# A two-layer attention kernel: v projected last, filling pieces spread from the first step to the last, and products between attention steps issued by column tiles

## The chip, the core and the metric

The kernel runs on one core of a Trainium2 chip, in float32 throughout. The metric is the device time of one execution in microseconds; a time is the median of several runs. The time before is 4138.08 us (three runs, 4136.69 to 4138.17). TensorE (`PE` in the profile) multiplies and writes to PSUM; ScalarE (`ACT`) applies functions such as Exp and copies; VectorE (`DVE`) adds, multiplies and takes reciprocals; `DMA` moves data between HBM and SBUF.

## What is computed

Sixteen images of 256 channels by 32 x 32 pixels go through two layers. An image is 1024 tokens of 256 channels.

```python
# layer 0: attention with 4 heads of 64
qkv = (xs @ w_proj + b_proj).reshape(B, S, N_HEADS, 3 * D_K)
q, k, v = jnp.split(qkv, 3, axis=-1)
attn = softmax(einsum('bihd,bjhd->bijh', q, k) * SCALE, axis=2)
res = einsum('bijh,bjhd->bihd', attn, v).reshape(B, S, N_HEADS * D_K)
res = res @ w_out + b_out + xs
# layer 1: group norm, attention with 8 heads of 32, group norm, MLP 256 -> 1024 -> 256
x = x + attention(group_norm(x, gn1_w, gn1_b), qkv_w, proj_w, proj_b, phys_bias)
h = group_norm(x, gn2_w, gn2_b)
h = gelu(einsum('oc,bchw->bohw', mlp_w1, h) + mlp_b1)
h = einsum('oc,bchw->bohw', mlp_w2, h) + mlp_b2
return x + h
```

## The kernel before

Tensors lie channels on partitions: an image is a tile `[128, 2, 1024]`. The keys of a block of 128 tokens, as the stationary operand, meet 512 query columns, so scores come out transposed, keys on partitions. Exp is taken straight from PSUM without a maximum; its result is the moving operand of the weighted sum with v. A test at the end of the kernel on the sums (`in_range`) decides whether a general, slower second pass is needed. It isn't with these inputs.

An attention runs in steps. A step computes the scores of one to three (item, key block) units, `s_a` in layer 0 and `s_b` in layer 1, and hands them to ScalarE for Exp; then it issues the weighted sums `acc_a` or `acc_b` of the step before. Each head takes its own rows of TensorE in the scores (D of 128) and its own columns in the weighted sums (D of 128), with D 64 in layer 0 and 32 in layer 1.

```python
        per = 6 // G                       # G = 128 // D heads side by side
        ...
        def scores(i, kb):
            t, c = items[i]
            tiles = [wide(f"s_{key}_{i}_{kb}_{n}") for n in range(G // 2)]
            for g in range(G):
                nc.tensor.matmul(          # L252
                    tiles[g // 2][:, g % 2, :],
                    kT[g * D : (g + 1) * D, c, kb * P : (kb + 1) * P],
                    qT[g * D : (g + 1) * D, c, t * TB : (t + 1) * TB],
                    start=True, stop=True,
                )
            ...
                nc.scalar.activation(e, s, AF.Exp, scale=scale)      # L264
        def weigh(i, kb, es):
            ...
            for g in range(G):
                nc.tensor.matmul(          # L273
                    accs[i][g * D : (g + 1) * D, :],
                    v_of(c * G + g, kb),
                    es[g // 2][:, g % 2, :],
                    start=(kb == 0), stop=(kb == SB - 1),
                )
            ...
                nc.vector.tensor_add(d, held[i][n] if kb == 1 else d, e)   # L290
        ...
        pending = []
        for step in steps:
            now = [scores(*u) for u in step]
            for p in pending:
                weigh(*p)
            pending = now
            yield
        for p in pending:
            weigh(*p)
        yield
```

`normalise` adds up the denominators with a product of ones (`den_a`, `den_b`, L300, also D columns wide) and divides. The PSUM tiles `wide` (two banks) rotate over three buffers: scores, projections and MLP outputs all take them in turn. `bank` tiles have two buffers.

The projections to q, k and v are six pieces, each with a `wide` tile. ScalarE takes q and k out of PSUM, VectorE takes v out.

```python
        def qk(ch, which, dst):
            ps = wide(f"qk_{key}_{ch}_{which}")      # four products 128 x 128 x 512, L406
            ...
        def v(half):
            ps = wide(f"v_{key}_{half}")             # eight products 128 x 128 x 256, L428
            ...
        pieces = [
            lambda: qk(0, 1, kT), lambda: qk(0, 0, qT), lambda: v(0), lambda: v(1)
        ]
        for ch in range(1, CC):
            pieces.append(lambda ch=ch: qk(ch, 1, kT))
            pieces.append(lambda ch=ch: qk(ch, 0, qT))
        return pieces
```

The driver fills the steps of the second attention of image b with whole pieces of other work: the eight pieces of the MLP's second product of image b-1 (`m`, L534, eight products of 128 x 128 x 256 each) and the six projection pieces of image b+1's first attention. `later.tick()` issues work that was put off by some steps: denominators, the output projections (`o`, `j`, L336) and the parts of group norm. Layer 1's own projections and the MLP's first product (`m`, L517) run outside the attentions' steps or after the first attention's last ones.

```python
    def run(stage, fill=None):
        for n, _ in enumerate(stage):
            later.tick()
            if fill and n in fill:
                fill[n]()
    ...
        fill = outputs + (first_qkv if b > 0 else [])
        tiles1, second_qkv = qkv_1(b, xn)
        run_pieces(second_qkv)
        hn = act.tile([P, CC, S], F32, tag="gn", name=f"hn_{b}")
        run(
            attention_1(...),
            {2 * n + 2: piece for n, piece in enumerate(fill)},
        )
        hidden, outputs = mlp(b, xs[b], hn)
```

The second attention has 32 units in steps of one, so steps 0 to 31 and a last one for the last weighted sums. With 14 pieces the places were steps 2, 4 ... 28; image 0 has none, image 15 has the eight `m` pieces alone.

Of the kernel before, what the change touches and what calls it, by code (L numbers as in the profile page):

```python
# [14 lines left out]
P = 128  # L15
# [175 lines left out]
def first_pass(ctx, tc, x, out, k):  # L191
    nc = tc.nc
    B, C, S = x.shape
    CC, SB, NT = C // P, S // P, S // TB
# [33 lines left out]

# [4 lines left out]
    def attention(layer, b, D, qT, kT, v_of, ones_of, scale, project):  # L238
        key = f"{layer}_{b}"
        G = P // D  # L240
        items = [(t, c) for t in range(NT) for c in range(CC)]
        units = [(i, kb) for i in range(len(items)) for kb in range(SB)]
        per = 6 // G
        steps = [units[n : n + per] for n in range(0, len(units), per)]
        res = act.tile([P, CC, S], F32, tag="res", name=f"res_{key}")
        accs, held, sums = {}, {}, {}
# [9 lines that stand above are left out]
                    start=True,  # L256
                    stop=True,
                )
            es = []
            for n, s in enumerate(tiles):  # L260
                e = work.tile(
                    [P, 2, TB], F32, tag="e", name=f"e_{key}_{i}_{kb}_{n}", bufs=8
                )
                nc.scalar.activation(e, s, AF.Exp, scale=scale)  # L264
                es.append(e)
            return i, kb, es

        def weigh(i, kb, es):
            t, c = items[i]
            if kb == 0:  # L270
                accs[i] = bank(f"acc_{key}_{i}")
# [5 lines that stand above are left out]
                    start=(kb == 0),  # L277
                    stop=(kb == SB - 1),
                )
            if kb == 0:  # L280
                held[i] = es
                return
            if kb == 1:
                sums[i] = [
                    work.tile([P, 2, TB], F32, tag="es", name=f"es_{key}_{i}_{n}", bufs=4)
                    for n in range(G // 2)
                ]
            for n, e in enumerate(es):
                d = sums[i][n]
                nc.vector.tensor_add(d, held[i][n] if kb == 1 else d, e)  # L290
            if kb == SB - 1:
                r = res[:, c, t * TB : (t + 1) * TB]
                nc.scalar.copy(r, accs.pop(i))
                later.after(2, lambda: normalise(i, r))

        def normalise(i, r):
            t, c = items[i]
            den = bank(f"den_{key}_{i}")
            for g in range(G):
                nc.tensor.matmul(  # L300
                    den[g * D : (g + 1) * D, :],
                    ones_of(c * G + g),
                    sums[i][g // 2][:, g % 2, :],
                    start=True,
                    stop=True,
                )
            at = next(block)
            d = work.tile([P, TB], F32, tag="d", name=f"d_{key}_{i}", bufs=1)
            nc.scalar.activation(  # L309
                d, den, AF.Identity, accum_out=dsum[:, at : at + 1]  # L310
            )
            nc.scalar.activation(
                den, den, AF.Exp, scale=-1.0 / DEN_MIN, accum_out=lsum[:, at : at + 1]
            )
            nc.vector.reciprocal(d, d)  # L315
            nc.vector.tensor_mul(r, r, d)
            if c == CC - 1:
                later.after(3, lambda: project(t, res))

        pending = []  # L320
        for step in steps:
            now = [scores(*u) for u in step]
# [4 lines that stand above are left out]
        for p in pending:  # L327
            weigh(*p)
        yield


    def out_proj(key, w, nk, src, bias, xs, t, stats):
        ps = wide(f"{key}_{t}")
        for co in range(CC):
            for kc in range(nk):
                nc.tensor.matmul(  # L336
                    ps[:, co, :],
                    w[:, kc, co * P : (co + 1) * P],
                    src(kc),
                    start=(kc == 0),  # L340
                    stop=(kc == nk - 1),
                )
        for co in range(CC):
            y = xs[:, co, t * TB : (t + 1) * TB]
            nc.vector.scalar_tensor_tensor(
                y, ps[:, co, :], bias[:, co : co + 1], y, ALU.add, ALU.add
            )
            if stats is not None:
                nc.vector.bn_stats(stats[:, co, t, :], y)


    def group_norm(key, src, stats, gw, gb, y):
# [10 lines left out]

        def variances():
            ps = bank(f"gm_{key}")
            nc.tensor.matmul(ps[:, :CC], k["gavg"], st["mean_c"], start=True, stop=True)
            mean = small.tile([P, CC], F32, tag="mean", name=f"mean_{key}")
            nc.vector.tensor_copy(mean, ps[:, :CC])

            dv = small.tile([P, CC], F32, tag="dv", name=f"dv_{key}")  # L370
            nc.vector.tensor_sub(dv, st["mean_c"], mean)
            nc.vector.tensor_mul(dv, dv, dv)
            tv = small.tile([P, CC], F32, tag="tv", name=f"tv_{key}")
            nc.vector.tensor_add(tv, dv, st["mv"][:, :, 1])
            st.update(mean=mean, tv=tv)
            later.after(1, apply)

        def apply():
            ps = bank(f"gv_{key}")
            nc.tensor.matmul(ps[:, :CC], k["gavg"], st["tv"], start=True, stop=True)  # L380
            rstd = small.tile([P, CC], F32, tag="rstd", name=f"rstd_{key}")
            nc.vector.tensor_scalar(rstd, ps[:, :CC], EPS, None, ALU.add)
            nc.gpsimd.tensor_tensor(rstd, rstd, k["mhalf"], ALU.pow)
            a = small.tile([P, CC], F32, tag="ga", name=f"ga_{key}")
            nc.vector.tensor_mul(a, rstd, gw)
            ma = small.tile([P, CC], F32, tag="gma", name=f"gma_{key}")
            nc.vector.tensor_mul(ma, st["mean"], a)
            c = small.tile([P, CC], F32, tag="gc", name=f"gc_{key}")
            nc.vector.tensor_sub(c, gb, ma)
            for t in range(NT):  # L390
                sl = slice(t * TB, (t + 1) * TB)
                for cc in range(CC):
                    nc.vector.tensor_scalar(  # L393
                        y[:, cc, sl], src[:, cc, sl],
                        a[:, cc : cc + 1], c[:, cc : cc + 1], ALU.mult, ALU.add,
                    )
# [4 lines left out]
    def qkv(key, D, src, weights, b_qk, b_v, v_op, qT, kT, v_dst):  # L401
        def qk(ch, which, dst):
            ps = wide(f"qk_{key}_{ch}_{which}")
            for t in range(NT):
                for cc in range(CC):
                    nc.tensor.matmul(  # L406
                        ps[:, t, :],
                        weights(cc, which)[:, ch * P : (ch + 1) * P],
                        src[:, cc, t * TB : (t + 1) * TB],
                        start=(cc == 0),  # L410
                        stop=(cc == CC - 1),
                    )
# [8 lines left out]
        def v(half):  # L421
            ps = wide(f"v_{key}_{half}")
            n = SB // 2
            for i in range(n):
                sb = half * n + i
                o = ps[:, i // 2, (i % 2) * C : (i % 2 + 1) * C]
                for cc in range(CC):
                    nc.tensor.matmul(  # L428
                        o,
                        src[:, cc, sb * P : (sb + 1) * P],  # L430
                        weights(cc, 2),
# [8 lines left out]
                v_op,  # L440
            )

        pieces = [
            lambda: qk(0, 1, kT), lambda: qk(0, 0, qT), lambda: v(0), lambda: v(1)
        ]
        for ch in range(1, CC):
            pieces.append(lambda ch=ch: qk(ch, 1, kT))
            pieces.append(lambda ch=ch: qk(ch, 0, qT))
        return pieces

    def qkv_0(b, xb):
        q = act.tile([P, CC, S], F32, tag="q0", name=f"q0_{b}")
# [56 lines left out]
    def mlp(b, xb, hn):  # L509
# [20 lines left out]
        def reduce(t, co, half):  # L530
            n = TB // 2
            ps = wide(f"m2_{b}_{t}_{co}_{half}")[:, 0, :n]
            for hc in range(HC):
                nc.tensor.matmul(  # L534
                    ps,
                    k["w2"][:, hc, co * P : (co + 1) * P],
                    gs[t, hc][:, half * n : (half + 1) * n],
# [42 lines left out]
    for b in range(B):  # L580
# [12 lines left out]
        if b + 1 < B:  # L593
            tiles0, first_qkv = qkv_0(b + 1, xs[b + 1])
        run_pieces(first_qkv if b == 0 else hidden)
        later.flush()
        fill = outputs + (first_qkv if b > 0 else [])
        tiles1, second_qkv = qkv_1(b, xn)
        run_pieces(second_qkv)
        hn = act.tile([P, CC, S], F32, tag="gn", name=f"hn_{b}")  # L600
# [4 lines left out]
                    f"h{b}", xs[b], st, k["g2w"], k["g2b"], hn  # L605
                ),
            ),
            {2 * n + 2: piece for n, piece in enumerate(fill)},
        )
        hidden, outputs = mlp(b, xs[b], hn)  # L610
    later.flush()
# [296 lines left out]
```

## Time and profile before

| what | value |
|---|---|
| time, median of 3 | 4138.08 us |
| span of the profiled run | 4135.9 us |
| mean granted TensorE clock | 0.992 |
| PE busy | 4072.8 us, 18,817 matmuls |
| DVE busy | 2489.1 us |
| ACT busy | 2082.1 us |
| second attention, Exp (L264, `e_b`) | 1024 of 1022 ns |
| second attention, sums of Exp (L290, `es_b`) | 896 of 1216 to 1222 ns |
| `m`, 128 x 256 columns (L534) | 2048 matmuls, 474.7 us busy |
| data moved by DMA | 40.90 MB, mean 10 GB/s |

A line of a group names the source line, engine and operation, what is written from what, the shape (rows * columns of the stationary operand, then partitions x elements of the moving one) and the count; then busy time and mean duration of one; then the idle time just before such instructions and who ended it. Matmuls overlap, so their mean durations add up to more than their busy time. On the timeline equal instructions in a row are merged into one line: start, length, count, and in brackets the idle time before with its releaser. The end of a matmul is modelled, so differences between starts are the safer measure.

### The profile page before, as it was taken

How to read it: one execution, taken by the hardware profiler on the slowest of the kernel's cores; microseconds unless marked ns; L12 is line 12 of the kernel's file. 1: busy time of each engine (PE TensorE's matmuls, PEld its weight loads, DVE VectorE, ACT ScalarE, POOL GpSimd, SP SyncE). 2: the span in 40 equal slices, each digit the busy share in tenths (PEclk: the TensorE clock that was granted, in tenths of full speed). 3: DMA queues.
4: the chain of work that ended last, by engine and by line, in shares of the span. 5: the costliest groups of instructions: out<-in, count | busy, mean ns of one | idle time of the engine just before them, and what ended most of it. 6: DMA issues, size and time to landing. Idle time of an engine off the chain costs nothing.

```text
span 4135.9 us, 45760 instructions
## 1 busy us (share of the span) xinstructions
PE 4072.8 (98%) x18817; PEld 1689.5 (41%) x18817; DVE 2489.1 (60%) x2538; ACT 2082.1 (50%) x2623; POOL 32.7 (1%) x54
## 2 busy tenths in 40 slices
PE   9999999999999999999999999999999999999998
PEld 3334344343443434434344343443434434344344
DVE  4684746747467474664746647466574665737563
ACT  4564545545455454554545545454454544645452
POOL 1000000000000000000000000000000000000000
PEclk9999999999999999999999999999999999999999
DMA  2000000000000000000000000000000000000000
GB/s 73 1 1 8 13 1 21 1 8 13 1 21 1 8 13 1 21 1 13 9 3 19 1 21 1 3 19 1 21 1 3 19 1 21 1 6 6 0 11 11
DMA packets 19800, 40.90 MB, mean 10 GB/s; under 512 B 5216, under 2 KB 6752, under 8 KB 19584
## 3 DMA queue, kind: packets, MB, share of 16 engines
q1 hardware_dynamic: 13824, 33.56, 2.2%
q10 hardware_dynamic: 5296, 4.20, 0.4%
q8 instruction: 149, 2.44, 0.2%
q14 instruction: 67, 0.55, 0.0%
q0 software_dynamic: 464, 0.15, 0.0%
HBM read 21.12 MB, written 16.78 MB: 9 GB/s over the span
## 4 chain that ended last, share of the span: by engine, by line
PE 91%; DVE 4%; ACT 2%; issue 2%; DMA 0%; POOL 0%; ACTq 0%; POOLq 0%; DVEq 0%
PE s_b L252 12%; PE acc_a L273 11%; PE m L517 11%; PE s_a L252 11%; PE acc_b L273 11%; PE m L534 10%; PE qk_a L406 6%; PE qk_b L406 5%; PE v_a L428 3%; PE o L336 3%; PE j L336 3%; PE v_b L428 3%; DVE es_b L290 2%; DVE d_b L315 2%; PE den_a L300 1%
## 5 line engine op out<-in xcount | busy, mean ns | idle before, releaser
L264 ACT ACTIVATE e_b<-s_b 128x1024 f32<-128x1024 f32 x1024 | 990.8, 1022 | 635.5 <-PE s_b L252 620.9
L290 DVE TENSOR_TENSOR es_b<-es_b,e_b 128x1024 f32<-128x1024 f32 x768 | 894.5, 1216 | 256.9 <-ACT e_b L264 256.4
L252 PE MATMUL s_b<-q,k 32*128 32x512 f32 x4096 | 647.3, 652 | 26.0 <-ACT e_b L264 18.1
L264 ACT ACTIVATE e_a<-s_a 128x1024 f32<-128x1024 f32 x512 | 488.6, 1024 | 199.0 <-PE s_a L252 168.7
L273 PE MATMUL acc_b<-e_b,v 128*32 128x512 f32 x4096 | 570.4, 615 | 1.6
L252 PE MATMUL s_a<-q,k 64*128 64x512 f32 x2048 | 490.9, 608 | 0.0
L290 DVE TENSOR_TENSOR es_a<-es_a,e_a 128x1024 f32<-128x1024 f32 x384 | 467.3, 1217 | 36.7 <-ACT e_a L264 10.6
L273 PE MATMUL acc_a<-e_a,v 128*64 128x512 f32 x2048 | 478.3, 601 | 0.0
L517 PE MATMUL m<-hn,w 128*128 128x512 f32 x1024 | 474.7, 605 | 2.0 <-DVE hn L393 2.0
L534 PE MATMUL m<-g,w 128*128 128x256 f32 x2048 | 474.7, 385 | 0.0
L534 PEld LDWEIGHTS m<-g,w 128*128 128x128 f32 x2048 | 379.1, 190 | 149.4 <-issue 66.9
L252 PEld LDWEIGHTS s_b<-q,k 32*128 32x128 f32 x4096 | 200.5, 186 | 398.5 <-issue 260.7
L525 ACT ACTIVATE g<-m,m1b 128x512 f32<-128x512 f32 x256 | 170.2, 685 | 314.2 <-PE m L517 313.8
L252 PEld LDWEIGHTS s_a<-q,k 64*128 64x128 f32 x2048 | 181.8, 186 | 282.0 <-issue 250.3
L290 DVE TENSOR_TENSOR es_b<-e_b,e_b 128x1024 f32<-128x1024 f32 x128 | 151.1, 1222 | 237.4 <-ACT e_b L264 237.4
L517 PEld LDWEIGHTS m<-hn,w 128*128 128x128 f32 x1024 | 186.0, 190 | 256.3 <-issue 190.7
L315 DVE RECIPROCAL d_a<-d_a 128x512 f32<-128x512 f32 x64 | 214.6, 3353 | 86.0 <-ACT d_a L309 86.0
L273 PEld LDWEIGHTS acc_a<-e_a,v 128*64 128x64 f32 x2048 | 131.3, 136 | 325.3 <-issue 320.7
L273 PEld LDWEIGHTS acc_b<-e_b,v 128*32 128x32 f32 x4096 | 83.0, 108 | 413.9 <-issue 385.4
L406 PE MATMUL qk_a<-x,wp 128*128 128x512 f32 x512 | 237.7, 608 | 8.1 <-DMA wp<-in_L_conv_w_proj_dram 8.1
L406 PE MATMUL qk_b<-xn,wq 128*128 128x512 f32 x512 | 229.2, 596 | 2.3 <-DVE xn L393 2.3
L315 DVE RECIPROCAL d_b<-d_b 128x512 f32<-128x512 f32 x64 | 214.2, 3346 | 2.7 <-ACT d_b L309 2.7
(104 smaller groups left out, 2290.5 us busy)
## 6 DMA issues: line engine op xcount, KB each, us to landing
x<-in_x_dram SPq DMA_DIRECT2D x32, 512.0 KB, 4.4
out_dram<-x SPq DMA_DIRECT2D x64, 256.0 KB, 2.0
w<-in_L_conv_mlp_w_dram ACTq DMA_DIRECT2D x2, 1024.0 KB, 11.4
wp<-in_L_conv_w_proj_dram ACTq DMA_DIRECT2D x6, 128.0 KB, 8.2
wq<-in_L_conv_qkv_w_dram ACTq DMA_DIRECT2D x1, 768.0 KB, 10.4
wo<-in_L_conv_w_out_dram ACTq DMA_DIRECT2D x1, 256.0 KB, 5.4
wpj<-in_L_conv_proj_w_dram ACTq DMA_DIRECT2D x1, 256.0 KB, 10.8
bv<-in_L_conv_b_proj_dram POOLq DMA_DIRECT2D x1, 128.0 KB, 8.0
```

The source lines that it names most:

```text
L252: nc.tensor.matmul(tiles[g // 2][:, g % 2, :], kT[g * D : (g + 1) * D, c, kb * P : (kb + 1) * P], qT[g * D : (g + 1) * D, c, t * TB : (t + ...
L264: nc.scalar.activation(e, s, AF.Exp, scale=scale)
L273: nc.tensor.matmul(accs[i][g * D : (g + 1) * D, :], v_of(c * G + g, kb), es[g // 2][:, g % 2, :], start=(kb == 0), stop=(kb == SB - 1),)
L290: nc.vector.tensor_add(d, held[i][n] if kb == 1 else d, e)
L300: nc.tensor.matmul(den[g * D : (g + 1) * D, :], ones_of(c * G + g), sums[i][g // 2][:, g % 2, :], start=True, stop=True,)
L315: nc.vector.reciprocal(d, d)
L336: nc.tensor.matmul(ps[:, co, :], w[:, kc, co * P : (co + 1) * P], src(kc), start=(kc == 0), stop=(kc == nk - 1),)
L406: nc.tensor.matmul(ps[:, t, :], weights(cc, which)[:, ch * P : (ch + 1) * P], src[:, cc, t * TB : (t + 1) * TB], start=(cc == 0), stop=(cc ...
L428: nc.tensor.matmul(o, src[:, cc, sb * P : (sb + 1) * P], weights(cc, 2), start=(cc == 0), stop=(cc == CC - 1),)
L517: nc.tensor.matmul(ps[:, n, :], k["w1"][:, cc, hc * P : (hc + 1) * P], hn[:, cc, t * TB : (t + 1) * TB], start=(cc == 0), stop=(cc == CC - 1),
L525: nc.scalar.activation(g, ps[:, n, :], AF.Gelu, bias=k["m1b"][:, hc : hc + 1])
L534: nc.tensor.matmul(ps, k["w2"][:, hc, co * P : (co + 1) * P], gs[t, hc][:, half * n : (half + 1) * n], start=(hc == 0), stop=(hc == HC - 1),)
```

## The change

Three things are changed. First, the projection pieces come in the order k, q, k, q, v, v instead of k, q, v, v, k, q, in both layers. Second, the pieces that fill the second attention stand evenly from step 0 to step 31, the last at step 31: with 14 pieces at 0, 2, 4, 7, 9 ... 28, 31. Third, while an attention's steps run, every other product goes through a helper that cuts the stationary operand's 128 columns into tiles of D columns, the width of the weighted sums, so that consecutive groups keep one shape of TensorE's array. Outside of the steps the helper issues full products as before.

```diff
+    cols = [P]
+
+    def product(o, w, r, **flags):
+        for c0 in range(0, P, cols[0]):
+            sl = slice(c0, c0 + cols[0])
+            nc.tensor.matmul(o[sl], w[:, sl], r, **flags)
 ... in attention()
+        cols[0] = D
         pending = []
         for step in steps:
 ...
             weigh(*p)
         yield
+        cols[0] = P
 ... in out_proj, in group_norm's two averages, in qk, in v and in the MLP's reduce
-                nc.tensor.matmul(
+                product(
 ... in qkv()
-        pieces = [
-            lambda: qk(0, 1, kT), lambda: qk(0, 0, qT), lambda: v(0), lambda: v(1)
-        ]
-        for ch in range(1, CC):
+        pieces = []
+        for ch in range(CC):
             pieces.append(lambda ch=ch: qk(ch, 1, kT))
             pieces.append(lambda ch=ch: qk(ch, 0, qT))
-        return pieces
+        return pieces + [lambda: v(0), lambda: v(1)]
 ... in the loop over images
+        last = NT * CC * SB - 1
-            {2 * n + 2: piece for n, piece in enumerate(fill)},
+            {n * last // max(len(fill) - 1, 1): piece for n, piece in enumerate(fill)},
```

More of the change, by code (lines that the diff above doesn't have):

```diff
@@ L365, in variances @@
             ps = bank(f"gm_{key}")
-            nc.tensor.matmul(ps[:, :CC], k["gavg"], st["mean_c"], start=True, stop=True)
+            product(ps[:, :CC], k["gavg"], st["mean_c"], start=True, stop=True)
             mean = small.tile([P, CC], F32, tag="mean", name=f"mean_{key}")
@@ L379, in apply @@
             ps = bank(f"gv_{key}")
-            nc.tensor.matmul(ps[:, :CC], k["gavg"], st["tv"], start=True, stop=True)
+            product(ps[:, :CC], k["gavg"], st["tv"], start=True, stop=True)
             rstd = small.tile([P, CC], F32, tag="rstd", name=f"rstd_{key}")
@@ L405, in qk @@
                 for cc in range(CC):
-                    nc.tensor.matmul(
+                    product(
                         ps[:, t, :],
@@ L427, in v @@
                 for cc in range(CC):
-                    nc.tensor.matmul(
+                    product(
                         o,
@@ L533, in reduce @@
             for hc in range(HC):
-                nc.tensor.matmul(
+                product(
                     ps,
```

## The prediction, made before the changed kernel was run

> **What bounds the kernel now.** I read the page first: the busy shares, the chain that ended last, and the costliest groups. `PE` is TensorE's matmuls, `PEld` its weight loads; a group line gives the shape of one instruction, the count, and then the busy time and the mean ns of one.
>
> ```profile
> PE 4072.8 (98%) x18817; PEld 1689.5 (41%) x18817; DVE 2489.1 (60%) x2538; ACT 2082.1 (50%) x2623; POOL 32.7 (1%) x54
> PE 91%; DVE 4%; ACT 2%; issue 2%; DMA 0%; POOL 0%; ACTq 0%; POOLq 0%; DVEq 0%
> L252 PE MATMUL s_b<-q,k 32*128 32x512 f32 x4096 | 647.3, 652 | 26.0 <-ACT e_b L264 18.1
> L273 PE MATMUL acc_b<-e_b,v 128*32 128x512 f32 x4096 | 570.4, 615 | 1.6
> ```
>
> TensorE is the bound: 98% busy, 91% of the chain. But 98% is not 98% useful. The count of matmul records is twice that of the program, so each float32 product is two passes. A pass over 512 columns takes 0.43 us: the steady weight loads of `qk_b` start at 2142.97, 2143.40, 2143.83 us. A pass over 256 columns takes 0.216 us: 30 of `v_b` between 2132.63 and 2139.11. Four of `acc_b`'s 32-column tiles, or four of `s_b`'s 32-row tiles, run at once, so eight of either are 0.86 us of work. All passes of the program so counted come to some 3,630 us, against 4,136 of span. The missing 500 us lie inside "busy", so I went to the timeline of TensorE over one middle image (columns: start, length, engine, line, operation). The images repeat every 256 us.
>
> ```profile
> 2211.12 1.06 PE L273 MATMUL acc_b<-e_b,v 128*32 128x512 f32 x8
> 2212.12 3.72 PE L534 MATMUL m<-g,w 128*128 128x256 f32 x16
> 2215.77 1.14 PE L252 MATMUL s_b<-q,k 32*128 32x512 f32 x8
> 2216.84 1.06 PE L273 MATMUL acc_b<-e_b,v 128*32 128x512 f32 x8
> 2217.72 1.04 PE L300 MATMUL den_b<-es_b,eones 128*32 128x512 f32 x8
> 2218.69 1.14 PE L252 MATMUL s_b<-q,k 32*128 32x512 f32 x8
> ```
>
> Read differences of starts, since ends are modelled. `acc_b` takes 1.00 us when a group of another shape follows and 0.88 when `den_b`, also 128*32, follows: leaving a shape costs 0.12. `m` takes 3.65 where 16 passes are 3.46: 0.19, about 0.10 for its first weights, which nothing hid, and 0.09 for leaving. So a group of full products put between the steps of an attention costs 0.19 us more than its passes, and the `acc_b` before it pays for leaving either way (scores would follow, also another shape).
>
> The second loss stands at both ends of the second attention.
>
> ```profile
> 2146.07 2.30 PE L252 MATMUL s_b<-q,k 32*128 32x512 f32 x12
> 2146.17 1.01 ACT L415 COPY q<-qk_b 128x1024 f32<-128x1024 f32 x1 [2.42 <-PE qk_b L406]
> 2147.20 1.28 ACT L264 ACT_TABLE_LOAD   x1
> 2148.50 3.77 ACT L264 ACTIVATE e_b<-s_b 128x1024 f32<-128x1024 f32 x4
> 2149.57 1.13 PE L252 MATMUL s_b<-q,k 32*128 32x512 f32 x4 [1.21 <-ACT e_b L264]
> 2150.63 1.83 PE L273 MATMUL acc_b<-e_b,v 128*32 128x512 f32 x8
> 2152.39 2.02 PE L252 MATMUL s_b<-q,k 32*128 32x512 f32 x8
> 2154.34 1.07 PE L273 MATMUL acc_b<-e_b,v 128*32 128x512 f32 x8
> ```
>
> The last `q` is copied out by ScalarE after the scores have begun, then the table for Exp is loaded, and only at 2148.50 does the first Exp run. The three score buffers are full and TensorE waits. From the first scores to the first filling piece (2155.33) are 9.26 us. The same 40 matmuls at their usual pace are 1.93 (sixteen scores in one go) + 1.00 + 1.07 + 1.00 = 5.00, so 4.26 us are lost.
>
> ```profile
> 2272.65 1.14 PE L252 MATMUL s_b<-q,k 32*128 32x512 f32 x8
> 2273.72 3.15 PE L273 MATMUL acc_b<-e_b,v 128*32 128x512 f32 x16
> 2276.80 2.85 PE L252 MATMUL s_a<-q,k 64*128 64x512 f32 x12
> ```
>
> At the end the last two steps' weighted sums take 3.08 us where 16 matmuls need 1.86 (0.43 x 4, 0.02, 0.12 for leaving): 1.22 us wait for the last Exps, with no piece left to fill.
>
> **What the Trainium skill says.** "TensorEngine Tiling (Array Packing)", Key Properties: a change of tiling mode, not of tile alone, drains the engine. The trace agrees: 0.12 us between `acc_b` and `m`, none between `acc_b` and `den_b`. "TensorE: Matmul & The Clock Gate", The mechanism: tiles in separate column groups run concurrently, a few ns apart. It agrees: eight `acc_b` of 615 ns each pass in 0.88 us. The same page, under "Wait — 56ns, not 53.3ns?", has matmuls start no closer than about 25 ns, however small; no run here comes near that, and it decides a rival below. "ScalarE: Activation LUTs", What ACT_TABLE_LOAD costs: about 1283 ns for the load itself; the trace has 1.28 us.
>
> **The change part by part**, per image of the regular kind (images 1 to 14), from the order of the built program and the rows above.
>
> (1) Column tiles. Within an attention every other product is cut into tiles of 32 columns (second attention) or 64 (first), the shape of the weighted sums. The matmul count rises fourfold or twofold, but the tiles run together, so I keep the pass times: a piece of `m` or `v_a` stays 16 x 0.216 = 3.46, one of `qk_a` or `j` 8 x 0.43 = 3.44. In the second attention 14 gaps per image held such products (`j` shared one). Each loses its 0.19 to 0.20 us: 14 x 0.196 = 2.74. Piece 0 now stands after the first scores with no weighted sum before it; where scores would have followed scores freely, there are two changes of shape, 0.35 us by the rows above (0.11 + 0.02 + 0.11 + 0.10). Net **2.4 us**. In the first attention `o` (between two weighted sums), `j` and one of group norm's small averages save 0.33 + 0.20 + 0.2: **0.7 us**.
>
> (2) v last. The order becomes k0, q0, k1, q1, v0, v1. ScalarE's last copy, and with it the table load, now come some 7 us (two `v_b` pieces of 3.46) before the first scores, and VectorE takes v out. Then Exp starts at once after the first scores, and piece 0 occupies TensorE for 3.46 us meanwhile. What stays is piece 0's buffer: it is that of v1, which VectorE frees 1.23 us (its eviction) after v1's end, while the first scores last 1.07 us: a wait of 0.2 to 0.4. The steady wait of 0.2 for a score group that no piece precedes (2209.88 to 2211.12 is 1.24 against 1.07) also stays. Gain 4.26 - 0.3 - 0.2 = **3.75 us**.
>
> (3) Last piece at step 31. It falls between the two last weighted sums, same shape on both sides, and covers the wait for the last Exps: **1.2 us**. The pieces are 2.4 steps apart instead of 2, so one more score group goes without a piece before it: **-0.2**.
>
> Sum: 2.4 + 0.7 + 3.75 + 1.2 - 0.2 = 7.85 us, times 14 images = 110. Image 0 has no pieces in its second attention and no table load there (1.4 us of wait before its first weighted sum): some 2, with a 1.3 us stall of `v_a` at 21.8 us in the first projection. Image 15 has eight pieces, all used by step 16 before and now spread to the end: about 7, by the same terms and part of the 2.99 us wait for `es_b` in the tail. Together about 119: 4138 - 119 = 4019. I say 4022, as small waits that I can't see only add.
>
> **Rivals.**
> A. Instruction supply. A tiled piece of 256 columns is 64 matmuls and 64 weight loads in 3.46 us, 27 ns for each instruction. The densest stretch in the trace, `acc_b` then `den_b`, is 32 in 1.85 us, 58 ns each, so nothing shows the rate needed. For it: group norm's `gv_g`, met with an empty queue, loads weights at 1604.12 and 1604.22 and the next ones follow at 1604.33; a pair per 0.105 us is an upper limit of 53 ns per instruction, and the matmul at 1604.15, 0.03 us after its load, hints at 30. At 53 ns ten pieces an image would each take 2 to 3 us longer: 20 to 30 us x 15, about 4,350 us. At 40 ns the gain of part 1 and more is gone, some 4,080.
> B. Tiles that don't overlap over a long chain. `acc_a` shows six pairs of passes at 0.43 each with two tiles, but chains of 16 with four tiles that read one moving operand are nowhere. If they ran even 10% slower, 14 x 0.35 = 5 us an image are lost: about 4,095.
> C. VectorE takes over the end. It needs 2 x 1.22 us per step in the second attention, and it evicts v1 and the last `m` just where buffers are scarce. Against it: 60% busy, and pieces spread evenly give it more time per step (2.4 x 2.1 + 3.5 = 8.5 us for 5.9 of sums). If it holds the first attention's third buffer, 1 us an image, 4,035.
> D. Only the order matters and the tiles neither gain nor cost: (2) and (3) alone, 4.75 x 14 + 8 = 75, 4,063.
>
> **Range and chances.** The gain from order (75 us, 1.8%) rests on waits that the timeline shows; the tiles add 45 us if their passes keep their pace. The limit for faster by over 2% is 4,055. Most of what can go wrong is A and B, which reach from 4,060 to 4,350; that the sum is too small by 25 us I also allow. Range 3,992 to 4,095; faster 0.68, within 0.20, slower 0.12.
>
> **What will show it.** In the timeline of a middle image: `acc_b` to a piece 0.88 us instead of 1.00; a piece of tiled `m` 3.46 to 3.6 instead of 3.65 to the next scores (if 4 or more, A or B); ACT_TABLE_LOAD before the first scores and the first weighted sum at its usual pace; from the first to the last scores no wait over 0.4 us; 16 `acc_b` at the end no longer one group of 3.08. An image then repeats every 248 us instead of 256. PEld's and PE's counts rise by some 9,100 (4,570 more products of two passes in the built program) to about 28,000, with little more busy time. The prediction is wrong if tiled pieces last longer than full ones, or if scores wait for VectorE's evictions of v.

## The result, and the profile after

The changed kernel takes 4013.68 us (median; 4011.88 to 4015.50), against 4137.91 before (the median of four executions now): a ratio of 0.970, 95% interval 0.9684 to 0.9717, or 124 us less. The prediction was 4022, range 3992 to 4095.

The page of the changed kernel has these lines, in the order in which the prediction read those of before (busy us, share, matmuls; then the chain; then two groups).

```profile
PE 3971.1 (99%) x27957; PEld 1518.4 (38%) x27957; DVE 2481.6 (62%) x2538; ACT 2078.1 (52%) x2623; POOL 32.7 (1%) x54
PE 94%; DVE 4%; issue 1%; ACT 0%; DMA 0%; POOL 0%; ACTq 0%; POOLq 0%; DVEq 0%
L262 PE MATMUL s_b<-q,k 32*128 32x512 f32 x4096 | 624.3, 640 | 2.8 <-DVE x L552 1.3
L236 PE MATMUL m<-g,w 128*32 128x256 f32 (+1 forms) x7808 | 464.9, 379 | 3.7 <-DVE v L448 3.7
```

There are 9,140 matmuls more and 102 us less of busy TensorE; ScalarE has left the chain (2% to 0%). The tiled `m` has four times the records, and about the same busy time as the full `m` had (474.7 us). All products that go through the helper carry its line, L236; the MLP's first product doesn't and keeps its own. The images repeat every 247.83 us (the second attention of images 7 and 8 begins at 1843.10 and 2090.93 us) where it was 255.97 (1890.10 and 2146.07).

The timeline of TensorE in the middle of the second attention, as before:

```profile
2099.21 1.06 PE L283 MATMUL acc_b<-e_b,v 128*32 128x512 f32 x8
2100.10 3.64 PE L236 MATMUL m<-g,w 128*32 128x256 f32 x64
2103.66 1.14 PE L262 MATMUL s_b<-q,k 32*128 32x512 f32 x8
2104.73 1.07 PE L283 MATMUL acc_b<-e_b,v 128*32 128x512 f32 x8
2105.73 1.37 PE L262 MATMUL s_b<-q,k 32*128 32x512 f32 x8
```

By starts, `acc_b` before `m` takes 0.89 us, about what it took before `den_b`; it still takes 1.00 before scores (2104.73 to 2105.73). `m` takes 3.56 to the next scores instead of 3.65: the change of shape on its way out, to the scores, is still paid.

The start of the second attention, with ScalarE and VectorE beside TensorE:

```profile
2084.13 1.01 ACT L427 COPY q<-qk_b 128x1024 f32<-128x1024 f32 x1 [2.42 <-PE qk_b L236]
2085.16 1.28 ACT L274 ACT_TABLE_LOAD   x1
2090.93 1.14 PE L262 MATMUL s_b<-q,k 32*128 32x512 f32 x8
2091.03 1.22 DVE L448 TENSOR_TENSOR v<-v_b,eones 128x1024 f32<-128x1024 f32 x1 [2.23 <-PE v_b L236]
2092.31 3.66 PE L236 MATMUL m<-g,w 128*32 128x256 f32 x64 [0.25 <-DVE v L448]
2095.91 1.14 PE L262 MATMUL s_b<-q,k 32*128 32x512 f32 x8
2096.98 1.06 PE L283 MATMUL acc_b<-e_b,v 128*32 128x512 f32 x8
```

The table load has ended four microseconds before the first scores, piece 0 follows them and waits 0.25 us for v's eviction, and the first weighted sum stands at its usual distance of 1.07 us from the second scores. At the end the two last weighted sums are parted by the last piece:

```profile
2208.78 1.07 PE L283 MATMUL acc_b<-e_b,v 128*32 128x512 f32 x8
2209.66 3.64 PE L236 MATMUL v_a<-wp,x 128*32 128x256 f32 x64
2213.11 1.04 PE L283 MATMUL acc_b<-e_b,v 128*32 128x512 f32 x8
2214.08 2.85 PE L262 MATMUL s_a<-q,k 64*128 64x512 f32 x12
```

The piece takes 3.45 us, its bare passes; the sums take 0.88 and 0.97. Nothing waits.

### The profile page after: what moved, and what is told of

Same layout as the page of the kernel before. It is cut to its first block, busy times and chain, and to the rows that moved or that the text cites. A ratio compares the mean times of both kernels' runs of the same rounds, so it can differ in the third digit from the quotient of the medians.

```text
span 4013.6 us, 64073 instructions
## 1 busy us (share of the span) xinstructions
PE 3971.1 (99%) x27957; PEld 1518.4 (38%) x27957; DVE 2481.6 (62%) x2538; ACT 2078.1 (52%) x2623; POOL 32.7 (1%) x54
## 4 chain that ended last, share of the span: by engine, by line
PE 94%; DVE 4%; issue 1%; ACT 0%; DMA 0%; POOL 0%; ACTq 0%; POOLq 0%; DVEq 0%
PE s_b L262 14%; PE acc_b L283 12%; PE m L527 11%; PE m L236 11%; PE s_a L262 11%; PE acc_a L283 11%; PE qk_a L236 6%; PE qk_b L236 6%; PE o L236 3%; PE v_b L236 3%; PE v_a L236 3%; PE j L236 3%; PE den_a L310 1%; PE den_b L310 1%; DVE d_a L325 1%
## 5 line engine op out<-in xcount | busy, mean ns | idle before, releaser
L262 PE MATMUL s_b<-q,k 32*128 32x512 f32 x4096 | 624.3, 640 | 2.8 <-DVE x L552 1.3
L283 PE MATMUL acc_b<-e_b,v 128*32 128x512 f32 x4096 | 546.1, 604 | 0.0
L527 PE MATMUL m<-hn,w 128*128 128x512 f32 x1024 | 476.1, 606 | 2.0 <-DVE hn L405 2.0
L236 PE MATMUL m<-g,w 128*32 128x256 f32 (+1 forms) x7808 | 464.9, 379 | 3.7 <-DVE v L448 3.7
L236 PEld LDWEIGHTS m<-g,w 128*32 128x32 f32 (+1 forms) x7808 | 272.6, 111 | 227.7 <-issue 59.3
L527 PEld LDWEIGHTS m<-hn,w 128*128 128x128 f32 x1024 | 186.6, 191 | 257.1 <-issue 191.5
L448 DVE TENSOR_TENSOR v<-v_b,eones 128x1024 f32<-128x1024 f32 x32 | 39.2, 1224 | 394.4 <-PE v_b L236 394.4
L236 PE MATMUL qk_a<-x,wp 128*32 128x512 f32 (+1 forms) x1856 | 234.3, 594 | 9.1 <-DMA wp<-in_L_conv_w_proj_dram 9.1
L236 PE MATMUL qk_b<-xn,wq 128*128 128x512 f32 x512 | 226.6, 596 | 3.3 <-DVE xn L405 3.3
```

Of the source, the lines that this page charges most:

```text
L236: nc.tensor.matmul(o[sl], w[:, sl], r, **flags)
L262: nc.tensor.matmul(tiles[g // 2][:, g % 2, :], kT[g * D : (g + 1) * D, c, kb * P : (kb + 1) * P], qT[g * D : (g + 1) * D, c, t * TB : (t + ...
L283: nc.tensor.matmul(accs[i][g * D : (g + 1) * D, :], v_of(c * G + g, kb), es[g // 2][:, g % 2, :], start=(kb == 0), stop=(kb == SB - 1),)
L448: nc.vector.tensor_tensor(v_dst[:, half * n : (half + 1) * n], ps.rearrange("p a (b h d) -> p (a b) h d", b=2, d=D), b_v.unsqueeze(1).to_b ...
L527: nc.tensor.matmul(ps[:, n, :], k["w1"][:, cc, hc * P : (hc + 1) * P], hn[:, cc, t * TB : (t + 1) * TB], start=(cc == 0), stop=(cc == CC - 1),
```

## The experiments

| run | median us | ratio to before | 95% interval |
|---|---|---|---|
| the change | 4013.68 | 0.9700 | 0.9684 to 0.9717 |
| tiles_alone | 4093.29 | 0.9892 | 0.9875 to 0.9908 |
| order_alone | 4065.29 | 0.9823 | 0.9806 to 0.9839 |
| no_v_last | 4027.47 | 0.9734 | 0.9718 to 0.9750 |
| no_spread | 4066.25 | 0.9829 | 0.9812 to 0.9845 |
| tiles_64 | 4045.47 | 0.9773 | 0.9758 to 0.9788 |
| narrow_128 | 4026.93 | 0.9729 | 0.9711 to 0.9746 |
| all_tiled | 4055.70 | 0.9798 | 0.9780 to 0.9816 |
| halves | 4050.74 | 0.9783 | 0.9770 to 0.9797 |
| qk_halves | 4016.33 | 0.9705 | 0.9692 to 0.9718 |
| qk_halves_v_mid | 4014.54 | 0.9700 | 0.9686 to 0.9713 |
| qk_halves_full | 4071.36 | 0.9839 | 0.9824 to 0.9854 |
| v_last_first_only | 4010.65 | 0.9688 | 0.9675 to 0.9702 |

All compute everything that the reference does. Edits are against the changed kernel. narrow_128 and all_tiled have two executions each, the others four or five. The kernel before took 4137.79 to 4139.79 beside them, so a difference of 2 us between two of these medians says nothing by itself.

### The parts by themselves

**tiles_alone**

```diff
-        return pieces + [lambda: v(0), lambda: v(1)]      # k q k q v v
+        return pieces                                     # k q v v k q, as before
-            {n * last // max(len(fill) - 1, 1): piece for n, piece in enumerate(fill)},
+            {2 * n + 2: piece for n, piece in enumerate(fill)},
```

> The change's column tiles alone, with the order of pieces and their places as before. Theory T (a change of the array's shape costs 0.19 to 0.20 us per gap, and tiles of the weighted sums' width avoid it): 14 gaps x 0.196 = 2.7 us per image in the second attention and 0.7 in the first, 3.4 x 14.5 = some 50 us, so 4088; the waits at the start (4.26 us) and end (1.22 us) of the second attention stay. Rival D (only the order matters): 4138. Were the tiles to run slower than full products, over 4138.

Measured 4093.29: 44.5 us less than before (4137.79 on that chip), where theory T had 50. Rival D, that only the order matters, falls. In the trace the waits at both ends stay as they were: 9.10 us from the first scores to the first piece (1871.52 to 1880.62), and one group of 3.08 us for the last weighted sums.

**order_alone**

```diff
-        cols[0] = D
+        cols[0] = P
```

> v last and pieces from step 0 to step 31, with full products of 128 columns everywhere. Theory T: the change less 3.4 us per image, 4014 + 50 = 4064; acc_b before m takes 1.00 us again, m 3.65 to the next scores. If the tiles gave nothing: 4014. If the two parts depend on each other (piece 0 and piece 31 cost more with two changes of shape, 0.3 us each): up to 4070.

Measured 4065.29, one microsecond from theory T's number. So the order is worth 72.5 us by itself and the tiles 51.6 on top of it. The two parts alone sum to 117 of the change's 124: they depend on each other little, by some 7 us. Its timeline at the end shows one place where they do: the last piece, full, between two weighted sums.

```profile
2238.61 1.07 PE L283 MATMUL acc_b<-e_b,v 128*32 128x512 f32 x8
2239.61 3.72 PE L236 MATMUL v_a<-wp,x 128*128 128x256 f32 x16
2243.26 1.06 PE L283 MATMUL acc_b<-e_b,v 128*32 128x512 f32 x8
```

1.00 + 3.65 us by starts, against 0.88 + 3.45 with tiles: 0.32 for the two changes of shape, in and out, with the first weights.

**no_v_last** and **no_spread** take one half of the reordering away each, and keep the tiles.

```diff
 no_v_last:
-        return pieces + [lambda: v(0), lambda: v(1)]
+        return pieces                                     # k q v v k q
 no_spread:
-            {n * last // max(len(fill) - 1, 1): piece for n, piece in enumerate(fill)},
+            {2 * n + 2: piece for n, piece in enumerate(fill)},
```

> The change without v last: tiles, and pieces from step 0 to 31, but k, q, v, v, k, q. Theory V (the prediction's step 2: v last frees the start of the second attention): the table load and the last copy of q stand again between the first scores and the first Exp, 2.3 us, so some 2 to 3.5 us per image are lost and the time is 4045 to 4065. Rival P (piece 0, which now stands right after the first scores and lasts 3.46 us, covers that wait by itself; v last then only replaces ScalarE's eviction by VectorE's before piece 0): within 0.3 us per image of the change, 4009 to 4019.

> The change with v last and tiles, but the pieces at steps 2, 4 ... 28 as before. Theory V: the start is nearly free, a wait of 1 to 1.5 us for the third buffer and the first Exps, and only the end's 1.2 us come back: 4014 + 14 x 2 = 4042. Rival P (piece 0 does the work at the start): the start loses 3 us or more, 4014 + 14 x 4.2 = 4073 or above.

Measured 4027.47 and 4066.25: neither theory's number in either case. The timelines say why. The start of the second attention without v last:

```profile
2096.63 1.14 PE L262 MATMUL s_b<-q,k 32*128 32x512 f32 x8
2097.76 1.28 ACT L274 ACT_TABLE_LOAD   x1
2097.80 3.66 PE L236 MATMUL m<-g,w 128*32 128x256 f32 x64
2101.39 1.14 PE L262 MATMUL s_b<-q,k 32*128 32x512 f32 x8
2102.46 1.06 PE L283 MATMUL acc_b<-e_b,v 128*32 128x512 f32 x8
```

The table load is back between the first scores and the first Exp, and costs nothing: from the first scores to the first weighted sum are 5.83 us, against 6.05 with v last. Rival P holds for the start; piece 0 covers the wait by itself. The 14 us of this run are lost elsewhere, late in the same attention:

```profile
2197.25 3.34 DVE L325 RECIPROCAL d_b<-d_b 128x512 f32<-128x512 f32 x1
2197.54 3.64 PE L236 MATMUL v_a<-wp,x 128*32 128x256 f32 x64
2203.32 1.21 DVE L448 TENSOR_TENSOR v<-v_a,bv 128x1024 f32<-128x1024 f32 x1
2204.59 1.14 PE L262 MATMUL s_b<-q,k 32*128 32x512 f32 x8 [1.35 <-DVE v L448]
```

With v in the middle, one `v_a` piece falls just after a block's denominators. VectorE divides for 3.34 us, has sums of Exp queued behind, and takes v out of PSUM 2.2 us after the piece's end (2201.11 to 2203.32); the scores that need that buffer wait 1.35 us. The trace has 14 such waits, 18.9 us in all; less the gain of 0.22 at each start that is 15.8, about the 14 measured.

In no_spread, v last alone brings the stretch from the first scores to the first piece from 9.10 us (tiles_alone) to 6.26 (2112.35 to 2118.61), of which 4.88 are work, the 5.00 less 0.12 that the tiles save. So v last takes 2.8 of some 4.2 us at the start, piece 0 takes all of it, and together they overlap. What this run loses, an image repeating every 251.11 us (1861.24 to 2112.35), is 3.3 us: the end's 1.2 (the last weighted sums are one group of 3.08 us again), some 0.7 at the start, and a wait of 1.27 us for an eviction of v behind a reciprocal, for the places of the pieces decide that too. Times 14 this is 46 of the 53 us; in the tail a wait of 3.0 us for `es_b` is back as well.

### What a change of shape costs

**tiles_64**

```diff
-        cols[0] = D
+        cols[0] = 64
```

> The change with products cut into tiles of 64 columns in the second attention too, where the weighted sums have 32. Theory T (a change of shape is what costs): each of about 14 gaps pays again 0.115 us for leaving the weighted sums' shape and 0.05 for the first weights of 64 columns, the last piece, between two weighted sums, 0.3: 2.4 us per image, 4014 + 34 = 4048. Rival (cutting in itself helps, for instance because narrow weights load quicker): within 8 us of the change.

Measured 4045.47, 32 us above the change, 3 from theory T. The timeline has the change's wait and the full products' one apart:

```profile
2116.05 1.07 PE L283 MATMUL acc_b<-e_b,v 128*32 128x512 f32 x8
2117.05 3.67 PE L236 MATMUL m<-g,w 128*64 128x256 f32 x32
2120.65 1.14 PE L262 MATMUL s_b<-q,k 32*128 32x512 f32 x8
```

1.00 us before a tile of another width, as before a full product; 3.60 for the piece, between the full product's 3.65 and the 3.56 of 32 columns. That the width of the first weights makes this small difference fits, but was not tested apart. It is the equal shape that pays, not the cutting.

### Whether tiles keep their pace

**narrow_128**: the MLP's second products on 128 moving columns.

```diff
-            for hc in range(HC):
-                product(ps, ..., gs[t, hc][:, half * n : (half + 1) * n], ...)
+            for z in range(2):
+                for hc in range(HC):
+                    product(ps[:, z * P : (z + 1) * P], ...,
+                            gs[t, hc][:, half * n + z * P : half * n + (z + 1) * P], ...)
```

> The change with the MLP's second products issued on 128 moving columns instead of 256, twice as many: 256 instructions per piece where the passes need 3.46 us, 13.5 ns each. It measures the rate at which instructions can be supplied and weights loaded (rival A). If neither limits: 4014. If the weight loads of some 110 ns set the pass: 32 passes of 0.11, +0.1 us a piece, 4026. If instructions come at 25 to 30 ns each: 256 of them take 6.4 to 7.7 us less a few queued ahead, +2.5 to 4 us a piece, 120 pieces: 4310 to 4500. At 53 ns: above 5,000.

Measured 4026.93. A piece:

```profile
2104.28 3.68 PE L236 MATMUL m<-g,w 128*32 128x128 f32 x128
2107.88 1.14 PE L262 MATMUL s_b<-q,k 32*128 32x512 f32 x8
```

128 matmuls and as many weight loads in 3.60 us are 14 ns for each instruction, twice the rate that the change needs, at 0.04 us more per piece. Rival A is out. Half of a 256-column pass would be 0.108 us, and a narrow weight load lasts 110 ns here, so the passes can't tell whether the loads would limit. The 13 us over the change fit the number for limiting loads, but only 5 of them lie in the pieces. The other 8 are waits of the scores for VectorE: 11.1 us in the trace (9.6 of them for `x`, the eviction of `m`) against 2.8 in the change. So the agreement with the number 4026 is largely chance.

**all_tiled**: tiles of 32 columns also outside of the attentions' steps.

```diff
-    cols = [P]
+    cols = [32]
-        cols[0] = P
+        cols[0] = 32
```

> The change with every helped product in 32-column tiles outside of the attentions too, so that long unbroken chains of tiled products stand in the trace: the v projections of the second attention (256 instructions in 6.9 us) and the last image's MLP (28 us). Rival B (long chains of tiles lag) or A (supply) would show passes of more than 0.216 us there: 0.25 would make v_b 8 us instead of 7. Theory T: the passes keep 0.216 and 0.43, and the time is the change's, plus up to 16 x 0.6 us for new changes of shape in the hidden stage: 4014 to 4025.

Measured 4055.70, above theory T's range. The pace isn't the reason. The longest unbroken chain, the last image's MLP, as far as the view goes (to 4048 us):

```profile
4022.27 26.10 PE L236 MATMUL m<-g,w 128*32 128x256 f32 x479
```

is 120 passes of four tiles in 26 us, 0.217 us each; rival B is out as well. What costs is the stage between the attentions, where the MLP's first product (L527) stays full and the scheduler mixes `o`, `qk_b` and group norm's averages into it: from the last weighted sum of the first attention to the first scores of the second it takes 59.02 us instead of 56.16. That is 2.86 us, nearly five times my allowance of 0.6; times 16 it is 46, for the 42 measured.

Besides changes of shape, single tiles cost here. Two of the scheduler's groups hold one column tile of a product alone:

```profile
2088.59 1.04 PE L236 MATMUL qk_b<-xn,wq 128*32 128x512 f32 x2
2089.56 1.98 PE L527 MATMUL m<-hn,w 128*128 128x512 f32 x4
```

Two matmuls are the two passes of one tile out of four, and they take 0.97 us, about what the whole product takes in the change (0.94, 2068.29 to 2069.23). The other three tiles follow after `m` and need the time again. `o` has the same at 2066.75. Two passes of 0.43 us lost twice are by estimate 1.7 of the 2.86 us. The tile that was put ahead keeps its lead to the end of `qk_b`:

```profile
2102.66 2.32 PE L236 MATMUL qk_b<-xn,wq 128*32 128x512 f32 x19
2104.40 0.59 PE L236 MATMUL v_b<-wq,xn 128*32 128x256 f32 x2
2104.80 0.60 PE L236 MATMUL qk_b<-xn,wq 128*32 128x512 f32 x3
2104.83 7.49 PE L236 MATMUL v_b<-wq,xn 128*32 128x256 f32 x126
```

It begins `v_b` 0.4 us before the other three have begun their last pass of `qk_b`, and doesn't wait for them. From its start `v_b` lasts 7.85 us (to the scores at 2112.25), which looks like the 8 us of rivals A and B. But the other three tiles can begin only at 2104.80 + 0.43 = 2105.23, and from there it is 7.02, where full products took 7.00. The pace is kept, and the lead is worth nothing, since the scores wait for the last tile.

### Finer pieces

**halves**, **qk_halves**, **qk_halves_v_mid**, **qk_halves_full**: the projection pieces in the second attention cut in two. halves cuts all six, qk_halves only those of q and k. qk_halves_v_mid is qk_halves (the "last run" of its text) with v in the middle in the second layer's own projections; qk_halves_full is qk_halves with full products.

```diff
-            for t in range(NT):
+            nt = NT // parts                         # parts = 2 for images from 2 on
+            ts = range(part * nt, (part + 1) * nt)
+            for t in ts:
 halves:
-        return pieces + [lambda: v(0), lambda: v(1)]
+        return pieces + [lambda half=half: v(half) for half in range(2 * parts)]
 qk_halves_v_mid:
+        at = 2 if D == D1 else len(pieces)
+        return pieces[:at] + [lambda: v(0), lambda: v(1)] + pieces[at:]
 qk_halves_full:
-        cols[0] = D
+        cols[0] = P
```

> The change with the six projection pieces that fill the second attention cut in halves (twelve of 1.72 us), so that 20 of 32 steps have a piece instead of 14. With tiles a gap costs nothing, so more gaps are free, and a score group that a piece precedes does not wait for its buffer (1.07 us against 1.24 to 1.30). Theory: 5 to 6 more score groups without the wait of 0.2, 1 us per image for images 1 to 14: 4000, less some for evictions in halves, which have a fixed part. If the wait for buffers is only moved: 4014.

Measured 4050.74, 37 us slower than the change instead of 14 faster. The halves of v begin earlier and meet a reciprocal again:

```profile
2216.77 3.35 DVE L325 RECIPROCAL d_b<-d_b 128x512 f32<-128x512 f32 x1
2222.84 0.68 DVE L451 TENSOR_TENSOR v<-v_a,bv 128x512 f32<-128x512 f32 x1
2223.58 1.93 PE L236 MATMUL v_a<-wp,x 128*32 128x256 f32 x32 [2.46 <-DVE v L451]
```

The next half waits 2.46 us for the buffer of the first, whose eviction stood behind the division, a multiplication and two additions. The trace has 14 such waits, 34.5 us of the 37.

> As in the run with halves, but only the four q and k pieces are cut in two and v stays whole and last, so that v's eviction no longer falls behind a reciprocal of 3.35 us on VectorE. Theory (that eviction was the loss; cutting as such gains): 18 pieces instead of 14, four more score groups at 1.07 instead of 1.24 us, 0.7 us per image: 4014 - 10 = 4004. Rival (more evictions on ScalarE cost what the gaps bring): 4014 or above.

Measured 4016.33. The loss of halves is gone, so that reading of it stands, but the gain of 10 us hasn't come either. The number is the rival's, but that evictions on ScalarE ate the gain is not shown. The timeline of the middle images gives another reason: of two score groups in a row without a piece only the first waits (in the change 2205.41 to 2206.71 is 1.30 us, the next, 2207.70 to 2208.78, 1.08). Parting such pairs by more pieces leaves the number of waiting groups much as it was: in one middle image's 32 score groups, 14 last over 1.1 us in the change and 15 in qk_halves. My count of gaps was not the count of waits.

> The last run, with v back in the middle for the second layer's own projections alone, where no reciprocal is in the way. The run without v last showed the start of the second attention 0.2 us shorter with v in the middle, since ScalarE frees piece 0's buffer sooner than VectorE: 0.22 x 15 = 3 us, 4001. Rival (the start needs v last after all): 4015 or above.

Measured 4014.54, 1.8 us below its sibling, with intervals that overlap; in the traces an image is 0.2 us shorter (247.96 against 248.17).

> The run with q and k in halves, with full products in place of tiles. Theory T: each of the four more gaps now costs two changes of shape, 0.2 us more, and saves a wait of 0.17: nothing is won, within 5 us of the order alone with full products, 4065. Rival (cutting pays whatever the shape): 4055.

Measured 4071.36, 6 us above the order alone with full products. As theory T has it, finer pieces win nothing there; they lose a little, one microsecond more than it allowed.

**v_last_first_only**

```diff
-        return pieces + [lambda: v(0), lambda: v(1)]
+        at = 2 if D == D1 else len(pieces)
+        return pieces[:at] + [lambda: v(0), lambda: v(1)] + pieces[at:]
```

> The change, but v last only in the first layer's projections, which fill the second attention; the second layer's own order is k, q, v, v, k, q again. If piece 0 alone frees the start of the second attention and v last pays only at the other place, by keeping v's eviction away from the reciprocals: the start gets 0.22 us shorter as in the run without v last, no 1.4 us wait comes back, 14 x 0.22 = 3 us less than the change: 4010 to 4012. If v last is needed at the start: 4016 or more.

Measured 4010.65, as piece 0's theory has it, and the fastest of all. Its interval overlaps the change's. In its trace an image repeats every 247.61 us (1839.82 to 2087.43), 0.22 less than in the change, and the first weighted sum stands 5.84 us after the first scores (2087.43 to 2093.27). v last has no use in the second layer's own projections; it has one in the pieces that fill the second attention.

## Why the prediction was right, point by point

- **TensorE's shape changes (step 1).** Right in mechanism and size: 3.1 us per image were predicted, about 45 us in all; the tiles measured 44.5 alone and 51.6 on top of the order. The 0.35 us that the step takes off for piece 0 belong to the order, since a full piece 0 changes the shape too. Without them its terms give 3.4 an image; the traces have 3.52 (an image repeats every 251.35 us in order_alone, 1866.79 to 2118.14). The 0.88 us before a piece came as stated, and 3.56 for `m` lies within the 3.46 to 3.6.
- **The start (step 2).** The size was right: the wait is gone but for piece 0's 0.25 us, predicted as 0.2 to 0.4. Its cause was put wrongly, and that the number came out is luck to this extent. I gave 3.75 us to v last, with piece 0 as a helper. no_v_last shows the start at full pace without v last, even 0.22 us shorter; no_spread shows that v last alone takes 2.8 of some 4.2. Two remedies for the same wait were counted as one, and the change has both. What v last does earn, about 14 us, is at a place that I had not looked at: VectorE's reciprocals.
- **The end (step 3).** Right: 1.22 us were to go, and the last two sums now take 0.88 and 0.97 us with no wait.
- **The sum.** 7.85 us per image were predicted, 8.14 measured (255.97 to 247.83). Images 0 and 15 missed in opposite directions, by some 2.5 and 4 us. In all 119 were predicted and 124 measured.
- **Image 0.** Wrong: some 2 us were to be saved and 0.55 were lost (the first attention of image 1 begins at 230.03 instead of 229.48 us). The stall of 1.3 us for `v_a` went, but the wait for the weights' transfer, which varies from 7.8 to 11.5 us over the runs, was 1.0 longer, so the first scores came only 0.2 us earlier. The wait before the second attention's first weighted sum stayed (149.62 to 152.93, against 149.16 to 152.46). And TensorE's wait for the first group norm grew by 1.0 us: the runs tell that this is v last in the first layer, for it is 3.3 to 3.5 us wherever v is last there and 2.3 before, in tiles_alone and in no_v_last. In the change VectorE takes v out at 120.03 and 123.70 us, 1.2 us each, between group norm's small operations.
- **Image 15.** Too small: 7 predicted, 11 measured (from the image's first scores to the end 323.5, then 312.5 us). The wait of 2.99 us for `es_b` in the tail went altogether, not in part.
- **Rivals.** A and B are refuted by the change itself, whose last piece takes its bare 3.45 us, and beyond its rate and length by narrow_128 and all_tiled. The floor of about 25 ns between starts, which was to decide A, doesn't hold between tiles. The trace of before had shown it: three of `acc_b`'s tiles begin within 0.02 us (626.67 to 626.69). A's 4,080 for 40 ns was also too low a sum: 128 instructions at 40 ns are 5.1 us, 1.7 more than a piece, 250 us over 150 pieces, less what is queued ahead. C, VectorE holding a buffer, didn't come about in the change, but it is what no_v_last, no_spread and halves ran into at another place: the risk was real and v's place avoids it. D is refuted by tiles_alone and order_alone.

## What to carry to other kernels

If TensorE is busy all the time and still above the sum of its passes, compare starts on the timeline group by group. Here the changes of the array's shape into a full product and out of it cost some 0.3 us together. A product cut into tiles of its neighbour's width avoids them at no loss of pace, but only on the side where the neighbour has that width: before scores the way out was still paid, and in tiles_64 the way in as well. See too that all tiles of a product stay together (all_tiled). Look at the two ends of a pipelined stage first when placing filling work; here 4.26 and 1.22 us of waiting stood there. And when a piece is put somewhere, look at which engine empties its buffer and what stands in that engine's queue at that moment: an eviction of v cost nothing or up to 2.5 us of TensorE's time, by what was ahead of it.

## What was not expected of the hardware

- Column tiles are not held together. In all_tiled one tile that was a product ahead began the next group 0.4 us before the other three had begun their last pass. One tile alone took as long as all four: 0.97 us for its two passes.
- TensorE took matmuls and weight loads at 14 ns per instruction over 256 in a row (narrow_128), and at 27 ns over 26 us (all_tiled: 958 instructions).
